# Seven block products for two node tiles in a relational graph layer, x kept in DRAM meanwhile, and eight buffers for the edge network

## The chip, the cores and the metric

The kernel runs on one core of a Trainium2 chip. The metric is device microseconds of one execution. The engines have these names in the profile: PE is TensorE (matrix products; PEld its loads of the stationary operand), DVE is VectorE, ACT is ScalarE, POOL is GpSimd, SP is SyncE, which issues most of the transfers here.

## What is computed (the reference, cut)

A stack of four graph layers ("blocks" 0 to 3) works on 1024 nodes with 512 features each and on 17408 edges, which are sorted by target node. Every layer first normalizes x and adds its result to x or replaces it. Block 0 is a convolution with a normalized adjacency matrix, block 1 multiplies gathered node features with weights that a small network makes for each edge (three products with SiLU between them), block 2 is a Chebyshev convolution. Block 3 is the one that the larger part of the change is about, a relational convolution, applied twice:

```python
def _rel_graph_conv(h, src, dst, etypes, norm, basis, comp, bias, loop_w, apply_relu):
    hb = jnp.einsum('nd,bdo->bno', h, basis)          # 4 bases of 512 x 512
    coef = comp[etypes]
    m = coef[:, 0, None] * hb[0][src]
    for b in range(1, basis.shape[0]):
        m = m + coef[:, b, None] * hb[b][src]
    m = m * norm[:, None]
    agg = jax.ops.segment_sum(m, dst, num_segments=n)
    out = agg + bias + h @ loop_w
    return jax.nn.relu(out) if apply_relu else out
```

The kernel changes the order: it sums the gathered rows of h for each basis first, and multiplies the sums with the bases afterwards. For a tile of 128 nodes that product is (128 x 2048) with (2048 x 512): 4 bases of 4 chunks of 128 each.

## The kernel before, in words

The code decides at run time between two arms, stack(True) and stack(False); the data of the runs takes the first (`fast`). All arithmetic that matters here is in float32. Instructions are traced in program order and then ordered by a planner, which lets an instruction go ahead when by its own cost estimates its inputs and buffers are ready; the order on each engine is then fixed. `pinned` and `issue_after` hold it to the traced order in places. A write at a place that is known only at run time counts as touching the whole tile.

**The edge network (L427 to L504).** `hidden` takes a batch of 1024 edges through three products (L434), each followed by a SiLU on ACT (L436) into a buffer of the tag `hid`, of which there are four. The third output is written to the table `hidtab` in DRAM (L438). Thirteen batches run two at a time (`in_turns`), one product between two groups of the loop that counts edges (L500, L504); the other four run later. The tiles for weights and edge data that later blocks need (`ew`, `ea`, `comps`, `w_mlp4`, `w_out0` and others, L106 to L118) lie in the pool `const` for the whole run; `load_rest` (L120) loads them.

**Rows.** `bias_row` (L93) loads a row of 512 numbers to all partitions. Rows share a tag of four buffers in `wpool`. Big weights (1 MB, `load_w`, L88) share another tag with four buffers there.

**Block 2** ends in `prop2` (L915): for each node tile, x is updated, normalized to h3, and h3 is written to the table `htabs[0]` (L919). `loop0` (L924) makes h @ loop_w plus the bias for a tile into `hb`, the tile `stage`.

**Block 3, layers l = 0 and 1 (L978 on).** The edges are cut into 68 groups of 256 (G = 2 times 128). For each group:

- `gathered` (L1001, gather at L279) fetches 2 x 128 rows of `htabs[l]` by indirect transfers that POOL issues, up to 11 buffers ahead;
- `weighted` (L1010) makes one-hot rows times coefficients on DVE (L1013);
- 8 products of 128 columns (16 instructions, L1027) sum the rows for four bases and a window of 32 nodes in a PSUM buffer `ps`, of which there are four;
- DVE adds them to `sums` (L1043), a tile [128, 4 chunks, 4 bases, 1024 nodes], at a column that is read from memory (`base(g)`).

Since the edges are sorted, a node tile n is complete when group `settled(n)` is through: 11, 19, 28, 36, 45, 53, 62 for tiles 0 to 6, and the end of the loop for tile 7. From then on `products` (L967) multiplies it with the four bases, 16 products of 512 columns (L972) into one PSUM bank, at most two products to a group; what is left runs after the loop (L1044). `ready` (L955) adds the result to `hb` (layer 0) or to x (layer 1). In layer 0 it then applies the relu on ACT, writes the tile to `htabs[1]` (L960) and lets POOL clear the tile's part of `sums` (L962); in layer 1 it writes the result out (L965).

In the first groups of either layer the loop products fill TensorE: tiles 3 to 7 of `loop0`, or of `turned5` and `loop1`, in groups 0, 1, 2, 4 and 6 (L1029). `loop1` adds into x on DVE and then the bias row on POOL (L990). Layer 1 begins with its weights (L980: loop weight, three bases, row; the fourth base at L982), whose buffers come free as layer 0's products finish with theirs, and with tiles 0 to 2 of `loop1`.

Of the kernel before, what the change touches and what calls it, by code (L numbers as in the profile page):

```python
# [21 lines left out]
P = 128  # L22
# [17 lines left out]
NY = 5  # L40
# [9 lines left out]
def gnn_stack(ctx, tc, a, out, xtab, htabs, hidtab):  # L50
# [42 lines left out]
    def bias_row(name, key):  # L93
        r = wpool.tile([P, D], F32, tag="row", name=f"row_{key}")
        nc.sync.dma_start(r, row_bcast(a[name], D))
        return r
# [8 lines left out]

    ew = const.tile([P, ET], F32, name="ew")  # L106

    ea = const.tile([P, ET, NY], F32, name="ea")

    comps = const.tile([P, 2, 8, NBAS], F32, name="comps")  # L110
    w_mlp2 = const.tile([P, P], F32, name="w_mlp2")
    w_mlp3 = const.tile([P, P], F32, name="w_mlp3")

    w_mlp4 = const.tile([P, 2, 4 * MUL], F32, name="w_mlp4")
    w_up0 = const.tile([P, MUL], F32, name="w_up0")
    w_up1 = const.tile([P, MUL], F32, name="w_up1")
    w_out0 = const.tile([P, 2, MUL], F32, name="w_out0")
    w_out1 = const.tile([P, 2, MUL], F32, name="w_out1")  # L118

    def load_rest():  # L120
        for t, key in ((w_up0, "L1_gnn_W_up0"), (w_up1, "L1_gnn_W_up1"), (w_mlp4, "L1_gnn_W_mlp4"), (ea, "edge_attr_4"),
                       (ew, "edge_weight")):
            nc.sync.dma_start(t, a[key])
        for t, key in ((w_out0, "L1_gnn_W_out0"), (w_out1, "L1_gnn_W_out1")):
            nc.sync.dma_start(t, a[key].rearrange("(c p) o -> p c o", p=P))
        for l in range(2):
            nc.sync.dma_start(comps[:, l], a[f"L3_gnn_comp{l}"])

        nc.gpsimd.tensor_scalar(w_out0[:, 1, :], w_out0[:, 1, :], 1.0 / math.sqrt(3.0), None, op0=ALU.mult)
# [233 lines left out]
    def stack(fast):  # L363
# [24 lines left out]

        cpool_cm = tc.tile_pool(name=f"cpool{fast}", bufs=1)
# [54 lines left out]
        def in_turns(batches):  # L444

            batches = list(batches)
            for i in range(0, len(batches), 2):
                pair = batches[i : i + 2]
                for _ in range(3):
                    for steps in pair:  # L450
# [4 lines left out]
                                 lambda q, i: l0.tile([P, 512], F32, tag="hid", name=f"hid_{q}_{i}", bufs=4))  # L455
# [386 lines left out]
        with tc.tile_pool(name=f"l2{fast}", bufs=1) as l2:  # L842
# [6 lines left out]
            b1 = bias_row("L2_gnn_b1", f"b1{fast}")  # L849
            gamma = bias_row("L2_gnn_gamma", f"gamma{fast}")  # L850
            beta = bias_row("L2_gnn_beta", f"beta{fast}")
            b2 = bias_row("L2_gnn_b2", f"b2{fast}")
# [90 lines left out]
        with tc.tile_pool(name=f"l3{fast}", bufs=1, reuse_waits="tile") as l3:  # L943
# [23 lines left out]
            def products(l, n, w3):  # L967

                po = bank2(f"po3_{l}_{n}")[:, 0, :]
                for b in range(NBAS):  # L970
                    for c in range(KC):
                        nc.tensor.matmul(po, sums[:, c, b, n * P : (n + 1) * P], w3[1 + b][:, c, :],  # L972
                                         start=(b == 0 and c == 0), stop=(b == NBAS - 1 and c == KC - 1))
                        if b == NBAS - 1 and c == KC - 1:
                            ready(l, n, po)
# [158 lines left out]
```

## Time and profile before

| what | value |
|---|---|
| median of 3 runs | 1245.97 us (1245.72 to 1247.47) |
| the profiled execution | 1234.54 us |
| its span (first to last instruction) | 1232.7 us |
| granted TensorE clock, mean | 0.997 |
| PE busy between 740 and 1230 us | nearly without a break |
| block 3, from the first group to the end | 712.7 to 1232.7 us |
| products with the bases in the chain that ended last | 17.8% of the span |
| edge groups (L1027) in that chain | 18.8% |

How to read the lines that follow in the prediction. The busy row gives for each engine its busy time, its share of the span and its number of instructions. The chain is followed backwards from the last instruction, at each step to whatever released it; in order of time its rows give start, length and what it was, "x8" meaning eight instructions in a row. A row of a group of instructions gives line, engine, operation, output and inputs with their shape and number, then busy time and the mean duration of one in ns, then idle time before them and what ended most of it. Durations of single matmuls overlap, so the distance from one start to the next is taken from rows with many in a row. A row of the waits gives who waited for whom, microseconds in total, times, and the longest. A row of the timeline gives start, length, engine, line, operation and form; an idle time before it stands in brackets.

### The profile page before, as it was taken

To read this page: it belongs to the slowest core of one execution; us is meant where nothing else is said; L and a number is where in the kernel's file an instruction comes from. 1 tells how busy PE (TensorE), PEld (TensorE's weight loads), DVE (VectorE), ACT (ScalarE), POOL (GpSimd) and SP (SyncE) were. 2 spreads that over 40 slices of the span, in tenths; PEclk is the share of its full clock that TensorE was granted. 3 is DMA by queue.
4 is the path that set the end of the run, shared out by engine and by line. 5 is a ranking of instruction groups with operands and counts; after the bars stand their busy time and mean duration, and the time that the engine had idled before them with its cause. 6 is when DMAs were issued, how large, how long until landed. Compare 5 with 4: busy or idle time off the path is not lost.

```text
span 1232.7 us, 17256 instructions
## 1 busy us (share of the span) xinstructions
PE 1203.1 (98%) x6338; PEld 799.5 (65%) x6354; DVE 617.2 (50%) x1180; ACT 291.2 (24%) x686; POOL 520.0 (42%) x596
## 2 busy tenths in 40 slices
PE   7988999999999999999999999999999999999998
PEld 3434567777777778544444567777776577777774
DVE  6877747777777676435443443333332143333331
ACT  4346254444444443322222400000000000000000
POOL 2000445666666662100000166565661486555530
PEclk9999999999999999999999999999999999999999
DMA  5171035444444441002002267555551666555540
GB/s 192 33 253 61 18 130 148 134 137 137 136 130 137 137 129 35 1 9 77 0 1 92 79 182 219 159 167 156 169 155 52 213 199 197 163 165 169 160 129 18
DMA packets 55620, 150.31 MB, mean 122 GB/s; under 512 B 8612, under 2 KB 10088, under 8 KB 55400
## 3 DMA queue, kind: packets, MB, share of 16 engines
q0 software_dynamic: 32640, 106.98, 30.3%
q1 hardware_dynamic: 22600, 41.63, 10.1%
q8 instruction: 52, 0.85, 0.3%
q10 hardware_dynamic: 288, 0.52, 0.1%
q14 instruction: 40, 0.33, 0.1%
HBM read 136.25 MB, written 12.85 MB: 121 GB/s over the span
## 4 chain that ended last, share of the span: by engine, by line
PE 93%; DMA 3%; ACT 1%; DVE 1%; issue 1%; POOL 1%; SPq 0%; ACTq 0%; DVEq 0%; POOLq 0%
PE ps L1027 19%; PE po L972 18%; PE pg L812 14%; PE pu L262 10%; PE pw L752 10%; PE pz L238 7%; PE py L238 4%; PE pl L238 4%; PE pm L434 3%; DMA hidtab_dram<-hid 2%; PE po L736 1%; PE pt_l L228 1%; PE pc L500 1%; PE pup L622 1%; PE pt_c L228 1%
## 5 line engine op out<-in xcount | busy, mean ns | idle before, releaser
L279 POOL DMA_INDIRECT m<-htab_dram,src_i x272 | 260.0, 956 | 167.4 <-PE ps L1027 115.9
L1027 PEld LDWEIGHTS ps<-wo,m 128*128 128x128 f32 x2176 | 261.5, 192 | 57.9 <-issue 56.2
L1027 PE MATMUL ps<-wo,m 128*128 128x128 f32 x2176 | 262.3, 275 | 1.0 <-DMA m<-htab_dram,src_i 1.0
L812 PEld LDWEIGHTS pg<-yo,msg 128*128 128x128 f32 x1632 | 192.8, 192 | 32.0 <-issue 16.3
L812 PE MATMUL pg<-yo,msg 128*128 128x32 f32 (+1 forms) x1632 | 187.8, 272 | 0.0
L1043 DVE TENSOR_TENSOR sums<-sums,ps 128x512 f32 x136 | 93.6, 688 | 157.3 <-PE po L972 133.8
L769 ACT ACTIVATE dot<-s,ea 128x128 f32<-128x128 f32 x408 | 130.0, 390 | 160.2 <-DVE msg L774 133.6
L279 POOL DMA_INDIRECT s<-xtab_dram,src_i x136 | 131.9, 970 | 37.3 <-issue 26.3
L752 PE MATMUL pw<-w_mlp,hq 128*128 128x512 f32 x272 | 133.3, 612 | 0.0
L1013 DVE TENSOR_TENSOR wo<-ohw,cwTrue 128x256 f32<-128x256 f16 x136 | 63.5, 469 | 103.5 <-PE ps L1027 103.5
L792 POOL TENSOR_TENSOR yo<-ohw,ea 128x160 f32<-128x160 f16 x136 | 63.2, 486 | 72.7 <-PE pg L812 72.7
L262 PE MATMUL pu<-parts,cnt 128*128 128x512 bf16 x373 | 84.1, 379 | 0.5
L953 POOL MEMSET sums<- 128x4096 f32 x1 | 3.5, 3512 | 165.8 <-PE pu L262 165.8
L752 PEld LDWEIGHTS pw<-w_mlp,hq 128*128 128x128 f32 x272 | 46.6, 191 | 33.5 <-issue 33.2
L262 PEld LDWEIGHTS <-cnt 128*128 128x128 f16 x384 | 37.6, 98 | 45.9 <-issue 3.4
L770 DVE TENSOR_TENSOR msg<-pw,s 128x512 f32<-128x512 f32 x68 | 47.0, 692 | 39.2 <-PE pw L752 36.4
L771 DVE TENSOR_TENSOR msg<-s,pw 128x768 f32<-128x768 f32 x68 | 64.2, 944 | 0.0
L972 PE MATMUL po<-basis_0True,sums 128*128 128x512 f32 x128 | 60.8, 600 | 0.2
L972 PE MATMUL po<-basis_3True,sums 128*128 128x512 f32 x128 | 59.8, 594 | 0.8 <-DVE sums L1043 0.8
L972 PE MATMUL po<-basis_2True,sums 128*128 128x512 f32 x128 | 59.9, 593 | 0.0
L972 PE MATMUL po<-basis_1True,sums 128*128 128x512 f32 x128 | 59.9, 593 | 0.0
L959 ACT ACTIVATE stage<-stage 128x512 f32<-128x512 f32 x8 | 5.0, 630 | 226.8 <-DVE stage L958 226.8
(175 smaller groups left out, 1284.0 us busy)
## 6 DMA issues: line engine op xcount, KB each, us to landing
hq<-hidtab_dram SPq DMA_DIRECT2D x17, 256.0 KB, 3.0
m<-htab_dram,src_i POOLq DMA_INDIRECT x272, 3.6
hidtab_dram<-hid SPq DMA_DIRECT2D x13, 256.0 KB, 4.1
s<-xtab_dram,src_i POOLq DMA_INDIRECT x136, 3.5
xtab_dram<-up SPq DMA_DIRECT2D x8, 256.0 KB, 2.0
basis_0True<-in_L_gnn_basis_dram SPq DMA_DIRECT2D x2, 1024.0 KB, 5.1
basis_1True<-in_L_gnn_basis_dram SPq DMA_DIRECT2D x2, 1024.0 KB, 5.2
htab_dram<-hl SPq DMA_DIRECT2D x8, 256.0 KB, 2.0
```

The source lines that it names most:

```text
L238: ins = nc.tensor.matmul(pz, hT[:, c, :], w[:, c, :], start=(c == 0), stop=(c == KC - 1)).ins
L262: nc.tensor.matmul(pu, m[:, s, d * P : (d + 1) * P], z[:, s, :], start=(s == 0 and j == 0), stop=(s == NB - 1 and j == len(zs) - 1))
L279: nc.gpsimd.indirect_dma_start(out=g, out_offset=None, in_=table, in_offset=bass.IndirectOffsetOnAxis(ap=idx[:, t : t + 1], axis=0))
L752: nc.tensor.matmul(pw[:, k, :], hq[q][:, (t % 4) * P : (t % 4 + 1) * P], w_mlp4[:, t // 4 % 2, :], start=True, stop=True)
L769: nc.scalar.activation(dot[:, k, m, :], s1[:, k, m, :], AF.Copy, scale=ea[:, g * G + k, 1 + m : 2 + m])
L771: nc.vector.tensor_mul(msg[:, :, 2:5, :], s1, w[:, :, 2:3, :].to_broadcast([P, G, 3, MUL]))
L792: nc.gpsimd.tensor_mul(yo[:, k], ohw[:, t, :].unsqueeze(1).to_broadcast([P, NY, W]), ea[:, t, :].unsqueeze(2).to_broadcast([P, NY, W]))
L812: nc.tensor.matmul(ps[:, b : b + n, :], lhsT, rhs, start=(k == 0), stop=(k == G - 1))
L972: nc.tensor.matmul(po, sums[:, c, b, n * P : (n + 1) * P], w3[1 + b][:, c, :], start=(b == 0 and c == 0), stop=(b == NBAS - 1 and c == KC ...
L1013: nc.vector.tensor_mul(wo, ohw[:, ts, :].unsqueeze(2).to_broadcast([P, G, NBAS, W]), cw[:, l, ts, :].unsqueeze(3).to_broadcast([P, G, NBAS ...
L1027: nc.tensor.matmul(ps[:, c * P : (c + 1) * P], m[k][:, c * P : (c + 1) * P], wo[:, k].rearrange("p b w -> p (b w)"), start=(k == 0), stop= ...
L1043: nc.vector.tensor_add(part, part, ps.rearrange("p (i w) -> p i w", w=W))
```

## The change

Five things are changed.

1. **Seven block products for two node tiles.** Two node tiles are taken together (`pair_products`). Their sums are a block matrix of two by two: rows are the two tiles, columns are bases 0 and 1, and bases 2 and 3. The bases are a block matrix of two by two too: rows are bases 0 and 1, and 2 and 3; columns are the left and the right 256 features. The product of the two is made by seven block products with sums and differences of blocks (the Winograd form of Strassen's scheme), not by eight. A block product is 2 bases x 4 chunks = 8 products of 256 columns. The differences of the bases (`Right.make`: t1 to t4, eight subtractions of 128 x 1024 a layer) are made once per layer on DVE, one to a group after group 8 (layer 0) or 10 (layer 1). t1 and t2 lie in the place of x (layer 0) or hb (layer 1), t3 overwrites a block of the bases, t4 has a tile. For each pair DVE makes s1, s2, s3 and s4 (128 x 1024 each; s3 and s4 overwrite blocks of `sums`) and adds every block product to one to four of the four result blocks.
2. **When the steps run.** A pair is begun when its second tile is settled (groups 19, 36, 53, and the end), and its 56 steps are spread evenly over the groups up to the next pair's beginning (`due`). The loop products move to groups 0, 2, 5, 8 and 11. `sums` is cleared for two tiles at a time; the last pair's part in group 4 of layer 1.
3. **x in DRAM.** In the fast arm `prop2` also writes x to `xtab`, and after the fourth block product of layer 0's last pair x is read back in eight transfers of 256 KB.
4. **Eight network buffers.** `hid` has eight buffers, not four.
5. **Places.** The tiles for weights and edge data move from `const` to a pool `early`, which is closed before block 3. The four rows of block 2 lie in block 2's pool `l2`; the tag of the other rows has two buffers. Layer 1's loop weight is asked for in group 12 of layer 0.

The diff, cut to its core:

```diff
-                                 lambda q, i: l0.tile([P, 512], F32, tag="hid", name=f"hid_{q}_{i}", bufs=4))
+                                 lambda q, i: l0.tile([P, 512], F32, tag="hid", name=f"hid_{q}_{i}", bufs=8 if fast else 4))
...
-            b1 = bias_row("L2_gnn_b1", f"b1{fast}")
+            b1 = bias_row("L2_gnn_b1", f"b1{fast}", l2)
...
                 h3[d] = normed(d, "l3")
+                if fast:
+                    nc.sync.dma_start(xtab[d * P : (d + 1) * P, :], x[:, d, :])
                 nc.sync.dma_start(htabs[0][d * P : (d + 1) * P, :], h3[d])
...
+            def cleared(p):
+                for n in (2 * p, 2 * p + 1):
+                    nc.gpsimd.memset(sums.rearrange("p c b d -> p (c b) d")[:, :, n * P : (n + 1) * P], 0.0)
...
+                def make(self):
+                    for b in range(HB):
+                        for out, x0, x1 in ((self.t1, self.block(0, 1), self.block(0, 0)), (self.t2, self.block(1, 1), self.t1),
+                                            (self.t3, self.block(1, 1), self.block(0, 1)), (self.t4, self.block(1, 0), self.t2)):
+                            nc.vector.tensor_sub(out(b), x0(b), x1(b))
+                            yield
+
+            PAIR = 7 * HB * KC
+
+            def pair_products(l, p, right):
+                a11, a12, a21, a22 = (left(p, i, j) for i in range(2) for j in range(2))
+                s1, s2 = (l3.tile([P, KC, HB, P], F32, tag=f"s{k}", name=f"s{k}_{l}_{p}") for k in (1, 2))
+                nc.vector.tensor_add(s1, a21, a22)
+                nc.vector.tensor_sub(s2, s1, a11)
+                s3, s4 = a21, a12
+                nc.vector.tensor_sub(s3, a11, a21)
+                two = bank2(f"po3_{l}_{p}")
+
+                h = (hb, x)[l][:, 2 * p : 2 * p + 2, :].rearrange("p i (k q) -> p (i k) q", k=2)
+                every, last3, lower, odd = slice(0, 4), slice(1, 4), slice(2, 4), slice(1, 4, 2)
+                for step, (lhs, rhs, places) in enumerate((
+                        (a11, right.block(0, 0), every), (a12, right.block(1, 0), slice(0, 1)), (s2, right.t2, last3), (s1, right.t1, odd),
+                        (s3, right.t3, lower), (s4, right.block(1, 1), slice(1, 2)), (a22, right.t4, slice(2, 3)))):
+                    ps = two[:, step % 2, step // 2 % 2 * H : (step // 2 % 2 + 1) * H]
+                    for b in range(HB):
+                        for c in range(KC):
+                            nc.tensor.matmul(ps, lhs[:, c, b, :], rhs(b)[:, c, :], start=(b == 0 and c == 0),
+                                             stop=(b == HB - 1 and c == KC - 1))
+                            if b == HB - 1 and c == KC - 1:
+                                part = h[:, places, :]
+                                nc.vector.tensor_add(part, part, ps.unsqueeze(1).to_broadcast([P, part.shape[1], H]))
+                                if step == 1:
+                                    nc.vector.tensor_sub(s4, a12, s2)
+                                if step == 3 and l == 0 and p == NB // 2 - 1:
+                                    for n in range(NB):
+                                        nc.sync.dma_start(x[:, n, :], xtab[n * P : (n + 1) * P, :])
+                                if step == 5:
+                                    ready(l, 2 * p)
+                                if step == 6:
+                                    ready(l, 2 * p + 1)
+                                    if l == 0 and p < NB // 2 - 1:
+                                        cleared(p)
+                            yield
+
+            since = [settled(2 * p + 1) for p in range(NB // 2 - 1)] + [NG]
+
+            def due(g):
+                return sum(max(0, min(PAIR, (g - a + 1) * PAIR // (b - a))) for a, b in zip(since, since[1:]))
...
-                        todo = (step for n in range(NB) for step in products(l, n, w3))
+                        right = Right(w3, (x, hb)[l], l)
+                        making = right.make()
+                        todo = (step for p in range(NB // 2) for step in pair_products(l, p, right))
...
-                            n = {0: 3, 1: 4, 2: 5, 4: 6, 6: 7}.get(g)
+                            n = {0: 3, 2: 4, 5: 5, 8: 6, 11: 7}.get(g)
...
-                            done = sum(settled(n) <= g for n in range(NB - 1))
-                            for _ in range(2):
-                                if given < done * NBAS * KC:
-                                    next(todo)
-                                    given += 1
+                            if l == 0 and g == 12:
+                                w3_1 = loop_weights(1)
+                            if l == 1 and g == 4:
+                                cleared(NB // 2 - 1)
+                            if g > 8 + 2 * l:
+                                next(making, None)
+                            while given < due(g):
+                                next(todo)
+                                given += 1
                             part = sums.rearrange("p c b d -> p (c b) d")[:, :, bass.ds(base(g), W)]
                             nc.vector.tensor_add(part, part, ps.rearrange("p (i w) -> p i w", w=W))
```

## The prediction

> **What bounds the kernel now.** I read the busy row first, then the chain that ended last, then the costliest groups.
>
> ```profile
> PE 1203.1 (98%) x6338; PEld 799.5 (65%) x6354; DVE 617.2 (50%) x1180; ACT 291.2 (24%) x686; POOL 520.0 (42%) x596
> ...
> PE 93%; DMA 3%; ACT 1%; DVE 1%; issue 1%; POOL 1%; SPq 0%; ACTq 0%; DVEq 0%; POOLq 0%
> ...
> L279 POOL DMA_INDIRECT m<-htab_dram,src_i x272 | 260.0, 956 | 167.4 <-PE ps L1027 115.9
> ...
> L972 PE MATMUL po<-basis_0True,sums 128*128 128x512 f32 x128 | 60.8, 600 | 0.2
> ```
>
> TensorE is the bound: 93% of the chain is its instructions, and it waits only some 25 us in all. So a microsecond of TensorE work taken out is a microsecond gained, unless TensorE then waits for something that its own work covers today. The gather row (L279) waits 115.9 us for TensorE: gathers are ahead, not late. The busy means (600 ns) overlap, so I take pitches from the chain in order of time, where only the extension counts:
>
> ```profile
> 56.94 7.22 DMA hidtab_dram<-hid
> ...
> 701.69 3.44 PE pl L238 x8
> ...
> 742.54 8.93 PE ps L1027 x80
> ...
> 947.38 17.35 PE po L972 x40
> ...
> 966.13 4.10 DMA htab_dram<-stage
> 973.55 3.68 DMA m<-htab_dram,src_i
> ```
>
> A product of 128x512 is two instructions of 3.44/8 = 430 ns; at 128 columns an instruction takes 8.93/80 = 111.6 ns. One edge group (L1027, 16 instructions) is thus 1.79 us, and a group with two products of L972 is 1.79 + 4 x 0.43 = 3.51 us.
>
> **Part 1, seven products for eight.** Removed: 2 layers x 8 tiles x 16 products = 512 instructions of 512 columns, 512 x 0.430 = 220.2 us (the chain has 17.8% of 1232.7 = 219.4). Added: 2 x 4 pairs x 56 products of 256 columns = 896 instructions. The trace has no f32 instruction of 256 columns. Below: half the 512 row, 215 ns; above: twice the 128 row, 223 ns. I take the line through both rows, 111.6 + 128 x (430 - 111.6)/384 = 217.7 ns, since both rows have a common overhead. 896 x 0.2177 = 195.1 us. **Gain 25 us**, bounds 20 (at 223) and 27.5 (at 215).
>
> The row at 512 columns is 430 ns against 111.6 at 128, so it is nearly in proportion to the columns. [...]
>
> **Part 2, eight network buffers.** The waits of TensorE and ScalarE before 102 us:
>
> ```profile
> PE pm L434 <- ACT hid L436: 7.0, 5, 2.7
> ```
> ```profile
> ACT hid L436 <- DMA hidtab_dram<-hid: 11.3, 4, 4.1
> ```
>
> TensorE's waits there are 2.00, 2.73 and 1.30 us, each behind a ScalarE output whose buffer is still being written to DRAM, and twice 0.46 in the odd last batch, which stay. A buffer comes round after 4 outputs, 4 x 1.08 = 4.3 us, and the write takes up to 7.2; with 8 it comes round after 8.7. **Gain 6.0 us.** VectorE is next: 37.7 us busy of 50 there, so the shorter stage (about 47 us of 53) still has room; bounds 3 and 6.
>
> **Part 3, tiles moved, rows in another pool, x through DRAM.** The early tiles' loads wait for the setup pool, finished before the branch: 0. The four bias rows now load after the last message group (478 us); the first is read after the product at 496.5 us, and a row lands in 3 to 6 us: 0, at most 2. x is written to DRAM eight times (256 KB, 2.0 us to landing) on SP, each ahead of the table write that layer 0's gathers wait for. The last is free 2.5 us before that write (704.69 us) and shares the engines with the basis_3 load issued at 699.45: 0.5 us, bounds 0 and 2.
>
> **Part 4, layer 0's groups.** Products now begin at group 19, not 11, so the gathers' pitch of 1.254 us (2.51 a group) against 1.79 could show. First gather 707.64, so the two of group 18 have landed at 707.64 + 37 x 1.254 + 3.68 = 757.7. TensorE starts group 0 at 712.7 and gets to group 18 after 18 x 1.79 + 5 loop products x 3.44 = 49.4, at 762.1. No stall. From 19 on a group has 3.29 steps of 2 x 0.2177: 1.79 + 1.43 = 3.22 us, over 2.51.
>
> Ahead of the first pair, VectorE makes the combined bases, 8 subtractions of 1024 elements (1.2 us each by the row fit below) from group 9 on (11 in layer 1). With the add (0.69) and the wo multiply (0.42) a group then takes VectorE about 2.1 us against 1.79; five such groups put it 1.6 us behind, which the four PSUM buffers of ps hide. Three of the eight need basis_2, whose load waits for the last loop product (issued at 742.57 today, landing in up to 9.0); that moves to 751.7 and lands by 761, ahead of group 21 (some 768), where the first product with it stands. Cost 0; up to 5 if VectorE's order has one of the three ahead of the adds.
>
> What is new in the loop is serial: each group's add into sums must follow that group's steps, and the next steps must follow that add, since the add's place is known only at run time. Memsets of sums stand in the same line, as today:
>
> ```profile
> 806.70 1.82 POOL L962 MEMSET sums<- 128x2048 f32 x1
> ```
> ```profile
> 808.55 1.41 DVE L1043 TENSOR_TENSOR sums<-sums,ps 128x512 f32 x2
> ```
> ```profile
> 806.00 3.96 PE L1027 MATMUL ps<-wo,m 128*128 128x128 f32 x34
> 810.01 1.98 PE L972 MATMUL po<-basis_0True,sums 128*128 128x512 f32 x4
> ```
>
> The add ran the moment the memset ended (808.52); TensorE filled the time with 34 instructions of later groups. For a pair the line is 17 x (steps 1.43 + end 0.16 + add 0.69 + restart 0.15) = 41.3; plus s1 to s3, 3 x 1.2 (rows 0.42, 0.69, 0.94 at 256, 512, 768 elements; 1.2 at 1024) less overlap, 3.4; s4 1.1; seven adds from PSUM 4.3; in layer 0 two memsets, 2 x 1.82 and their start, 4.2. That is 50.1 us in layer 1 and 54.3 in layer 0, against TensorE's 17 x 1.79 + 112 x 0.2177 = 54.8. TensorE stays the bound, narrowly. At a pair's end in layer 0, memset, add and s1 to s3 outlast three groups of cover (5.4 us, four PSUM buffers) by about 0.7 us: 2 x 0.7, and 1 for the first pair's start in each layer's loop and the rest: **2.5 us lost**, bounds 0 and 6 x 3.7 = 22 (no cover).
>
> Third pair, layer 0: it ends in the last group, so the memsets stand before the last add and the last pair's first product with no groups left: 2 x 1.82 + 0.69 + 0.2 = 4.5, less some transposes as cover: **4 us lost**, bounds 0 and 4.5. The last 56 steps then run back to back, 24.4 us, with s1 to s3 (3.4) under the first two products (7 us).
>
> **Part 5, between the layers.** Today the last product ends at 964.56, the table write is issued at 966.13, lands at 970.2, and gathering begins at 972.28. The 4 MB of weights had been issued 3.43 us apart, each landing in 5.1 to 5.4: no backlog. After the change 2 MB of x start 24 steps (10.4 us) before the end, then 1 MB each at 8.7, 6.9, 5.2 and 3.5 us before it. At some 390 GB/s (the best slices between 945 and 985 us show 385 to 408) 6 MB need 16 us, so the write waits to about 8.6 us after the end, not 5.6: **3 us lost**, bounds 0 and 8. The next layer's three loop products (11.6 us) cover the first part today and keep doing so.
>
> Layer 1's POOL also has the eight adds of the bias row (1.28 us) and, at group 4, the two memsets moved there, 1.68 each over a gather's pitch (805.75 to 808.68 less 1.25). Gather 37 is issued today at 1027.03, 54.75 after the first; with 3.4 for memsets and 3.68 to land, 61.8. TensorE without waiting gets to group 18 at 978.94 - 972.28 + 17 x 1.79 + 5 x 3.44 + 4 x 0.43 = 56.0. Products that today start at group 11 no longer cover this. 5.8, and some 0.2 more at group 19: **6 us lost**, bounds 2 and 9.
>
> **Sum**, against the profiled execution (1234.54, span 1232.7 and 1.8 around it): -25 - 6 + 0.5 + 2.5 + 4 + 3 + 6 = -15, so 1219.5. The runs' median, 1245.97, lies 0.9% above that execution; in proportion, 1245.97 x 1219.5/1234.54 = **1231 us**.
>
> **Rivals.** (a) The waits are covered: the order of the instructions fills them with later groups, as at 806 us. For it: only 1.0 us of waiting for gathers in all of today's trace. Against it: in layer 1 there is no work to fill with. 25 + 6 less 2 to 6: 1216 to 1221. (b) Slower: VectorE's line in the group loop becomes the bound. Place: groups 19 to 67 of both layers. Its margin is 0.5 us a pair in layer 0 and 4.7 in layer 1; each 0.1 us more per group adds 1.7 us a pair. At 0.5 us more (a wo multiply of 0.42, row L1013, in front of every add) a pair costs 8 in layer 0 and 3.8 in layer 1, 3 x 11.8 = 35, so 15 of gain turn into 20 of loss: 1266. It decides from about 0.3 us a group. For it: VectorE is busy 60% of the loop and serves in order. Against it: the multiply can run under TensorE's steps, as it does now. (c) The change doesn't do what it says: a 256-column instruction at 245 ns makes the products as dear as now; 6 less 16 is 10 lost, 1256. Both rows speak against it.
>
> **How the numbers follow.** Forecast 0.55 (own range 1222 to 1242), (a) 0.25, (b) 0.14, (c) 0.04, and 0.02 for a forecast that ends at no change. Range 1214 to 1247: from (a) with the low bound of part 1 to the forecast with part 5 at its high bounds (5 and 3 more) and 6 more in the loop; most of (b) and (c) is left out. Faster by over 0.2% (about what a measurement of this kernel can tell from no change) 0.80, within 0.04, slower 0.16.
>
> **What would show it.** Pitch of the new products at 215 to 223 ns; no wait of ScalarE for hidtab and pa starting near 96 us; memset, add and product in a row at layer 0's last pair, with TensorE idle some 4 us; layer 1's TensorE waiting for gathers around groups 12 to 19; the last htab write landing over 5 us after its issue. Wrong if TensorE idles within groups 20 to 66, behind the adds of sums.

## The result, and the profile after

The changed kernel takes 1268.03 us (median, 1265.27 to 1269.26) against 1246.20 for the kernel before in the same session: a ratio of 1.017, interval 1.015 to 1.019. It is slower by 1.7%; the forecast was 1231 us and faster.

The profile that came with this result, its busy row and the engines' shares of the chain:

```profile
PE 1197.9 (95%) x6722; PEld 883.0 (70%) x6738; DVE 691.5 (55%) x1268; ACT 291.1 (23%) x686; POOL 529.4 (42%) x596
...
PE 89%; DMA 4%; DVE 2%; issue 1%; ACT 1%; POOL 1%; another core or an unknown queue 0%; SPq 0%; ACTq 0%; DVEq 0%; POOLq 0%
```

TensorE is busy 5 us less than in the profile before (1197.9 against 1203.1), and the span is 32.4 us longer (1265.1 against 1232.7). So the products did become cheaper, and TensorE waits where it didn't wait before.

The two profiles can't be subtracted from one another, though. The runs fell on chips of two kinds: on some the kernel before takes about 1246 us, on others about 1236, and the profile that I predicted from (1234.5) is of the second kind while the three times shown beside it, and the profile after, are of the first. So I took both kernels once more on one chip of the second kind (c1_before, c2_after). There the medians are 1235.83 and 1246.24, and the changed kernel has a ratio of 1.0082 (1.0057 to 1.0108) to the kernel before: slower on that kind too, by 9 to 10 us. The readings below are of this pair unless they say otherwise. The busy rows, before and then after:

```profile
PE 1204.7 (98%) x6338; PEld 799.9 (65%) x6354; DVE 617.7 (50%) x1180; ACT 291.0 (24%) x686; POOL 517.7 (42%) x596
```
```profile
PE 1191.1 (96%) x6722; PEld 878.5 (71%) x6738; DVE 694.9 (56%) x1268; ACT 291.0 (23%) x686; POOL 529.2 (43%) x596
```

TensorE's work in block 3 can be counted from pitches: 112 instructions of 256 columns in a row take 24.43 us (a row shown under the first experiment), and in the undisturbed middle of that row 32 of them take 6.90 us from the first start to the start that follows them (timeline of c3_own_psum):

```profile
1208.30 7.07 PE L1039 MATMUL po<-stage,s 128*128 128x256 f32 x32
1215.20 1.89 PE L1039 MATMUL po<-basis_0True,sums 128*128 128x256 f32 x8
```

That is 0.2156 us from start to start; the sums here are made with 0.2155. The 896 new ones are 193.1 us, the 512 old ones 220.2 at 0.430. What TensorE's starts are apart beyond those pitches is waiting, or half clock. By stretch, in us, from profiles on chips of the second kind (the last three columns are experiments, told below):

| stretch of block 3 | before (c1) | changed (c2) | own PSUM (c3) | and VectorE clears (e6) | plain products (c8) |
|---|---|---|---|---|---|
| layer 0, groups 0 to 18 | 0.0 | 2.6 | 5.2 | 2.5 | 0.0 |
| layer 0, groups 19 to 66 | 2.2 | 6.3 | 3.8 | 3.8 | 0.4 |
| layer 0, last pair, and into layer 1 | 0.1 | 7.9 | 3.6 | 3.6 | 0.7 |
| layer 1, groups 0 to 18 | 0.9 | 12.4 | 13.4 | 5.0 | 6.8 |
| layer 1, groups 19 to 66 | -0.1 | 4.1 | 1.2 | 1.7 | 1.1 |
| layer 1, last pair | 1.0 | 8.3 | 1.7 | 1.7 | 1.7 |
| sum | 4.1 | 41.7 | 28.9 | 18.2 | 10.6 |

Before to changed: 27.1 us less work, 37.6 us more waiting, and block 3 begins 1.5 us earlier: +9.0, against +8.7 in the spans (1233.8 and 1242.5). The 1.5 is within what executions differ by: block 3 begins at 714.2 us in c1_before and at 712.7 and 713.1 in the two other profiles of the kernel before, and at 712.7 in c2_after. The gain is there in full, and more than that is lost to waits. Where the waits stand is read from the chain of c2_after at its end (start, length, what):

```profile
1207.68 3.71 PE po L1039 x16
...
1211.48 1.23 DVE x L1043
1212.71 0.04 issue
1212.76 3.73 PE po L1039 x16
...
1216.52 0.43 DVE x L1043
1216.95 0.04 issue
1216.99 3.73 PE po L1039 x16
1220.73 0.02 issue
1220.75 0.96 DVE x L1043
1221.71 0.04 issue
1221.76 3.73 PE po L1039 x16
```

Each block product (16 instructions) ends, VectorE adds it to one to four result blocks (0.43 to 1.23 us), and only then does the next one start. The rows of the waits sum this up (who waited for whom, total, times, longest):

```profile
PE po L1039 <- DVE x L1043: 5.1, 6, 1.4
...
PE pm L436 <- ACT hid L438: 4.9, 4, 3.2
PE po L1039 <- DVE stage L1043: 4.4, 5, 1.3
PE ps L1115 <- DVE sums L1135: 3.7, 1, 3.7
```

9.5 us stand in front of block products in the two last pairs. The row of `pm` shows that the wait for network buffers is still there with eight of them (6.1 us before). The last row is a wait in layer 1 that is read below.

### The profile page after: what moved, and what is told of

Read it like the earlier page. It is cut to its first block, busy times and chain, and to the rows that moved or that the text cites. A ratio compares the mean times of both kernels' runs of the same rounds, so it can differ in the third digit from the quotient of the medians.

```text
span 1265.1 us, 18143 instructions
## 1 busy us (share of the span) xinstructions
PE 1197.9 (95%) x6722; PEld 883.0 (70%) x6738; DVE 691.5 (55%) x1268; ACT 291.1 (23%) x686; POOL 529.4 (42%) x596
## 4 chain that ended last, share of the span: by engine, by line
PE 89%; DMA 4%; DVE 2%; issue 1%; ACT 1%; POOL 1%; another core or an unknown queue 0%; SPq 0%; ACTq 0%; DVEq 0%; POOLq 0%
PE ps L1115 19%; PE po L1039 16%; PE pg L814 14%; PE pu L237 10%; PE pw L754 10%; PE pz L213 7%; PE py L213 4%; PE pl L213 4%; PE pm L436 2%; PE po L738 1%; PE pt_l L203 1%; DMA types<-in_edge_type_dram 1%; DMA m<-htab_dram,src_i 1%; DMA hidtab_dram<-hid 1%; POOL sums L987 1%
## 5 line engine op out<-in xcount | busy, mean ns | idle before, releaser
L254 POOL DMA_INDIRECT m<-htab_dram,src_i x272 | 269.2, 990 | 159.1 <-PE ps L1115 100.9
L1115 PEld LDWEIGHTS ps<-wo,m 128*128 128x128 f32 x2176 | 269.3, 194 | 29.5 <-issue 8.9
L1115 PE MATMUL ps<-wo,m 128*128 128x128 f32 x2176 | 272.5, 278 | 15.0 <-remote 3.5
L794 POOL TENSOR_TENSOR yo<-ohw,ea 128x160 f32<-128x160 f16 x136 | 63.4, 488 | 72.3 <-PE pg L814 72.2
L1099 DVE TENSOR_TENSOR wo<-ohw,cwTrue 128x256 f32<-128x256 f16 x136 | 59.6, 440 | 49.0 <-PE ps L1115 41.8
L817 DVE TENSOR_TENSOR acc<-acc,pg 128x256 f32 x68 | 28.7, 422 | 48.5 <-PE pg L814 48.5
L1039 PE MATMUL po<-basis_0True,sums 128*128 128x256 f32 x128 | 33.7, 396 | 14.1 <-DVE sums L1135 11.1
L237 PE MATMUL pu<-parts,adj 128*128 128x512 bf16 x187 | 42.1, 379 | 3.7 <-ACT parts L244 2.3
L1039 PE MATMUL po<-basis_2True,sums 128*128 128x256 f32 x128 | 34.8, 400 | 7.5 <-issue 2.5
```

The costliest lines, as they stand in the source:

```text
L237: nc.tensor.matmul(pu, m[:, s, d * P : (d + 1) * P], z[:, s, :], start=(s == 0 and j == 0), stop=(s == NB - 1 and j == len(zs) - 1))
L254: nc.gpsimd.indirect_dma_start(out=g, out_offset=None, in_=table, in_offset=bass.IndirectOffsetOnAxis(ap=idx[:, t : t + 1], axis=0))
L794: nc.gpsimd.tensor_mul(yo[:, k], ohw[:, t, :].unsqueeze(1).to_broadcast([P, NY, W]), ea[:, t, :].unsqueeze(2).to_broadcast([P, NY, W]))
L1039: nc.tensor.matmul(ps, lhs[:, c, b, :], rhs(b)[:, c, :], start=(b == 0 and c == 0), stop=(b == HB - 1 and c == KC - 1))
L1099: nc.vector.tensor_mul(wo, ohw[:, ts, :].unsqueeze(2).to_broadcast([P, G, NBAS, W]), cw[:, l, ts, :].unsqueeze(3).to_broadcast([P, G, NBAS ...
L1115: nc.tensor.matmul(ps[:, c * P : (c + 1) * P], m[k][:, c * P : (c + 1) * P], wo[:, k].rearrange("p b w -> p (b w)"), start=(k == 0), stop= ...
```

## The experiments

Theory A: the products are cheaper as computed, and the waits have separate causes, which can be taken away one by one: (1) the PSUM buffer that a pair's seven block products share, (2) the combined bases that VectorE makes in order and the late load they need, (3) the two memsets in layer 1's group 4 and late gathers there. The rivals stand in the expectations.

**e1_own_psum**, a PSUM buffer for each block product:

```diff
-                two = bank2(f"po3_{l}_{p}")
...
-                    ps = two[:, step % 2, step // 2 % 2 * H : (step // 2 % 2 + 1) * H]
+                    ps = bank2(f"po3_{l}_{p}_{step}")[:, 0, :H]
```

> Each block product gets a PSUM buffer of its own (two in turn) in place of a quarter of one buffer per pair. Theory A (the waits in front of block products come from the shared buffer: a block product may not start before VectorE's add of the previous one): the waits behind the adds of L1043 go, 4.4 us in layer 0's last pair, 5.1 in layer 1's, 1.2 at the second block product of two pairs, so 11 to 13 us less than the changed kernel, ratio to the kernel before about 1.007. Rival (the waits are for something else of the previous block product, or the time is lost again behind other adds): under 3 us less, ratio 1.015 or more.

Measured: 1250.63 us, ratio 1.0044 (1.0027 to 1.0062). That is 17 us less than the changed kernel in the first session, 16 by the ratios, and more than theory A had counted. Once more, as the base of three others, on a chip of the second kind:

> The kernel with a PSUM buffer of its own for each block product once more, as the base of the next three on one chip. It was 1.0044 of the kernel before on a chip where the changed kernel was 1.017; on a chip where the changed kernel is 1.008 it should be 0.995 (theory A: 16 us of waits behind the shared buffer, whatever the chip). Rival (the gain was the chip's): nearer to 1.004 than to 0.995 there.

Measured: 1230.93 us, ratio 0.995 (0.9934 to 0.9965); the changed kernel has 1.0082 on such chips, so again 16 us less. The chain at the end of c3_own_psum:

```profile
1201.32 24.43 PE po L1039 x112
```

Where c2_after had seven pieces with VectorE between them, there is one of 112 instructions. The waits that go in the table are 10.9 us in the last pairs and 5.4 in groups 19 to 66. (The span of c3_own_psum is only 13.0 us shorter than that of c2_after, since the first groups of either layer wait 3.6 us more there.) In the last pairs they are the pieces shown above. In the groups of c2_after they can't be pointed at: TensorE has just two longer waits in front of a block product there, 0.87 us each at the beginning of a pair, which stay with own buffers, and all others are at most 0.14 us. Only in the first profile of the changed kernel do two second block products wait visibly (1.27 and 1.19 us). For the last pairs the cause is shown: with a buffer of its own a block product doesn't wait for the add, and in the shared one it did, although it wrote to other columns than the add read.

**e2_late_making**, in layer 0 the three subtractions that need basis_2 behind the adds of groups 15, 16 and 17; the edit also lets all eight begin after group 17 in program order, not after group 8:

```diff
-                            nc.vector.tensor_sub(out(b), x0(b), x1(b))
+                            with tc.issue_after(added[14 + k].ins) if l == b == 0 < k else nullcontext():
+                                nc.vector.tensor_sub(out(b), x0(b), x1(b))
...
-                            if g > 8 + 2 * l:
+                            if g > (17 if l == 0 else 10):
...
+                            added.append(nc.vector.tensor_add(part, part, ps.rearrange("p (i w) -> p i w", w=W)))
```

> The three subtractions that need basis_2 in layer 0 are held behind VectorE's adds of groups 15, 16 and 17. Theory A (VectorE stands 4.2 us before the load of basis_2, with the adds of sums behind it, and TensorE runs dry and falls to half clock): TensorE's idle 3.5 us at 767 to 771 us and half of the 3.4 us at half clock go, 5 to 6 us less than the changed kernel, ratio about 1.012 to 1.013. Rival (that stretch is limited by gathers, so the time comes back before group 19): 0 to 2 us less, ratio 1.015 to 1.017.

Measured: 1274.53 us, ratio 1.0227 (1.0204 to 1.025), 6 us more than the changed kernel. Neither expectation held. In the changed kernel's first profile VectorE's idle time before the subtraction is 3.24 us, not 4.2. TensorE's idle 3.5 us at 770 us went (layer 0's groups 0 to 18 wait 8.4 us, not 11.9 as in the changed kernel's first profile), but groups 19 to 66 wait 24.1, not 12.6, 5.4 of them in one piece, at 799.9 us, for an add whose own release the profile doesn't name. This fell on a chip of the first kind, and the changed kernel's first profile, from that kind too, has such a piece as well (5.50 us before 1068.5); what the edit alone costs stays open.

**e3_hid4**, four network buffers again (`bufs=8 if fast else 4` to `bufs=4`), and once more beside its base:

> Part 2 undone: four network buffers. Theory A (the eight buffers brought 0.5 us, since ScalarE still waits for table writes that stand behind other loads): within 2 us of the changed kernel, ratio 1.015 to 1.019. Rival (they bring the 6 us that the prediction counted, and other stages ate it): 4 to 6 us more than the changed kernel, ratio 1.020 to 1.022.

> The changed kernel once more, as the base of the next two on one chip: 1.008 of the kernel before where semaphores come in time, 1.017 on a chip like the first.

> Part 2 undone once more, beside its base. Theory A (the table writes stand behind big loads with eight buffers too, so the wait only moves): within 2 us of the changed kernel. Rival (the 6 us of the prediction are there): 4 to 6 us more.

Measured: 1270.12 us, ratio 1.0203 (1.018 to 1.0226). In the second session the changed kernel has 1269.60, 1.0186 (1.0159 to 1.0213), and four buffers 1270.71, 1.0197 (1.0169 to 1.0225). The first ratio falls at the low end of the rival's range, but its interval reaches the changed kernel's; the second, taken side by side, is theory A's: 1.1 us.

In their own stage the eight buffers did bring something. `pa`, the first product behind it, starts at 97.3 to 101.2 us in the 13 profiles with eight buffers (mean 99.1) and at 101.4 to 102.7 in the five with four (mean 102.1). That is 3 us, half of the forecast. At the first product of the message groups, near 185 us, the means differ by only 1.2 us. What became of the rest of the wait can be read from the chains. Before (c1_before), then changed (c2_after):

```profile
56.93 7.12 DMA hidtab_dram<-hid
...
64.75 7.00 DMA hidtab_dram<-hid
```
```profile
57.12 13.03 DMA types<-in_edge_type_dram
70.16 4.88 DMA w_out<-in_L_gnn_W_out_dram
75.11 8.65 DMA hidtab_dram<-hid
```

With four buffers two table writes of 7 us hold ScalarE. With eight, ScalarE runs on, and what it then waits for is a later write. Two rows of c2_after:

```profile
SPq L385 <- DMA types<-in_edge_type_dram: 5.3, 1, 5.3
ACT hid L438 <- DMA hidtab_dram<-hid: 6.2, 2, 4.3
```

SyncE, which issues loads and table writes in one line, waits 5.3 us until a load has landed before it issues the next one. The write comes behind that one, takes 8.65 us, and ScalarE waits 4.3 us for it. Between 55 and 85 us the hardware queue's packets fill 82% of the 16 engines' time at 250 GB/s in the first profile before and 79% at 223 GB/s in the first profile after. That the queues are the limit there, and not the number of buffers, fits this, but no run tests it.

**e4_plain_pairs**, the schedule of the changed kernel (pairs, `due`, moved loop products, memsets, x in DRAM) with ordinary products; sums, differences and combined bases are left out:

```diff
-            PAIR = 7 * HB * KC
+            PAIR = 2 * NBAS * KC
...
+            def pair_plain(l, p, w3):
+                for n in (2 * p, 2 * p + 1):
+                    yield from products(l, n, w3)
...
-                        todo = (step for p in range(NB // 2) for step in pair_products(l, p, right))
+                        todo = (step for p in range(NB // 2) for step in pair_plain(l, p, w3))
```

> The schedule of the changed kernel (pairs from groups 19, 36, 53 and the end, moved loop products, memsets by pairs, x in DRAM) with ordinary products of 512 columns, 32 to a pair, without sums, differences and combined bases. Theory A (the seven products save 27 us of TensorE's time, and about 20 us of that are lost to waits that the block products bring with them, the rest of the loss being the schedule's): 220 - 193 = 27 more, 12 less for the shared PSUM buffer, 5 for the making, 3 for s1 to s3, so 5 to 9 us more than the changed kernel, ratio 1.021 to 1.025. Rival (the products as blocks save nothing on the chip, their extra work on VectorE is the whole loss): faster than the changed kernel by 10 us or more, ratio under 1.009.

> The schedule of the changed kernel with ordinary products of 512 columns, without sums, differences and combined bases, beside its base. Theory A (27 us less work by seven products, 16 us of which are lost to the shared PSUM buffer and some 5 to sums, differences and combined bases; the schedule alone costs some 15 us of waits): 4 to 8 us more than the changed kernel, ratio 1.011 to 1.015. Rival (the schedule costs next to nothing where semaphores come in time, the blocks' waits eat the whole gain): ratio 1.000 to 1.004, 5 us or more less than the changed kernel.

> The pair schedule with ordinary products once more. On a chip where the kernel before takes about 1237 us theory A expects a ratio of 1.011 to 1.015 (the schedule alone costs some 15 us), the rival 1.000 to 1.004. On a chip with 1246 us it is 1.016 again.

Measured: 1265.51 us, ratio 1.0168 (1.0144 to 1.0192), and 1266.07, 1.0159 (1.0131 to 1.0187), on chips of the first kind; 1240.31 us, 1.0039 (1.0023 to 1.0056), on one of the second. None of the three fell where theory A had it: I expected the schedule to cost some 15 us by itself, and on the second kind of chip it costs 5. There the rival of c8 held, 6 us less than the changed kernel: as written, the block products lose more than they save. That they save nothing on this chip, the rival of e4, is refuted by c3_own_psum, which is 9 us under plain products with the same schedule.

**e5_loops_early, e6_clear_dve, e7_both**, on own PSUM buffers. e5 puts the loop products back, e6 clears the last pair's part of `sums` on VectorE behind layer 0's last product, e7 does both:

```diff
-                            n = {0: 3, 2: 4, 5: 5, 8: 6, 11: 7}.get(g)
+                            n = {0: 3, 1: 4, 2: 5, 4: 6, 6: 7}.get(g)
```
```diff
-                                    if l == 0 and p < NB // 2 - 1:
-                                        cleared(p)
+                                    if l == 0:
+                                        cleared(p, nc.gpsimd if p < NB // 2 - 1 else nc.vector)
...
-                            if l == 1 and g == 4:
-                                cleared(NB // 2 - 1)
```

> Own PSUM buffers, and the loop products of tiles 3 to 7 back in groups 0, 1, 2, 4 and 6, as before the change. Theory A (the moved loop products hold the buffer that basis_2 needs; its load comes at group 12, stops the gathers for some 4 us and VectorE waits for it with the adds of sums behind it): basis_2 lands before VectorE asks for it, 3 to 5 us less than the base. Rival (the cover is only used up earlier, TensorE then waits for gathers before group 19): within 1 us of the base or slower.

> Own PSUM buffers, and the last pair's part of sums cleared for layer 1 by VectorE behind layer 0's last product, not by GpSimd in group 4 of layer 1. Theory A (GpSimd's two memsets, 3.6 us in the line of its gathers, hold the adds of sums at about group 7 and make the gathers late afterwards): TensorE's idle 3.7 us and the half clock behind it go, and part of the later waits for gathers, 6 to 10 us less than the base. Rival (layer 1 is bound by its gathers with or without the memsets): 0 to 3 us less.

> The last two together on own PSUM buffers. Theory A (three separate causes): the gains of both add up, 9 to 15 us less than the base, ratio to the kernel before 0.983 to 0.988 where the base has 0.995. Rival (both act on the same wait for gathers): no better than the better of the two by more than 1 us.

Measured against c3_own_psum (1230.93) on the same chip: 1229.31 us, ratio 0.9944 (0.9926 to 0.9962); 1225.05, 0.991 (0.9876 to 0.9944); 1223.93, 0.9901 (0.9883 to 0.9919). e6 is 6 us less by the medians, at the low end of what theory A had, though its interval and that of c3_own_psum overlap a little. What it takes away is read from the timeline of c2_after (start, length, engine, line, form, idle before it):

```profile
1000.71 3.56 POOL L987 MEMSET sums<- 128x2048 f32 x2
1004.31 1.41 DVE L1135 TENSOR_TENSOR sums<-sums,ps 128x512 f32 x2 [8.18 <-POOL sums L987]
...
1005.05 6.36 PE L1115 MATMUL ps<-wo,m 128*128 128x128 f32 x32 [3.72 <-DVE sums L1135]
```

The memsets stand behind gathers and a bias add in GpSimd's order and start at 1000.7; the add of a group, already computed, waits 8.2 us for them; the four PSUM buffers of `ps` fill, and TensorE idles 3.7 us. The 32 instructions that follow take 6.36 us, not the 3.6 of their pitch: the granted clock was 0.5 from 1003.5 to 1010.4 us. Without these memsets layer 1's groups 0 to 18 wait 5.0 us, not 13.4.

The memsets are only about half of what is lost there. Of the 12.4 us of c2_after, 6.5 are in groups 6 to 8, where the memsets stand, and 5.7 in groups 16 to 18. (The plain pairs of c8, with the same memsets, lose 5.5 in groups 6 to 8: that is most of what the schedule costs by itself.) In groups 16 to 18 it is the load of basis_2, in layer 1:

```profile
1032.36 1.23 DVE L1016 TENSOR_TENSOR stage<-basis_2True,stage 128x1024 f32<-128x1024 f32 x1 [2.96 <-DMA basis_2True<-in_L_gnn_basis_dram]
1036.89 7.22 PE L1115 MATMUL ps<-wo,m 128*128 128x128 f32 x48 [2.85 <-issue]
```

VectorE waits 2.96 us for the load and does three subtractions before the next add; TensorE idles 2.85 us, and the clock is at half for 3.41. In e6 VectorE still waits 2.6 us for the load, but TensorE by then waits for gathers (2.0 us at 1021); its waits in groups 15 and 16 are 3.9 us together.

e5 is 1.6 us less by the medians, between the two expectations and with intervals that overlap. What the load of basis_2 does in layer 0 is the same. VectorE of c2_after:

```profile
755.67 0.42 DVE L1099 TENSOR_TENSOR wo<-ohw,cwTrue 128x256 f32<-128x256 f16 x1
758.28 1.23 DVE L1016 TENSOR_TENSOR x<-basis_2True,x 128x1024 f32<-128x1024 f32 x1 [2.19 <-issue]
759.42 1.22 DVE L1016 TENSOR_TENSOR basis_0True<-basis_2True,basis_0True 128x1024 f32<-128x1024 f32 x1
760.56 1.22 DVE L1016 TENSOR_TENSOR t<-basis_2True,x 128x1024 f32<-128x1024 f32 x1
761.69 0.68 DVE L1135 TENSOR_TENSOR sums<-sums,ps 128x512 f32 x1
```

VectorE stands 2.2 us before the subtraction that needs basis_2, and does three in a row before the next add; TensorE, four PSUM buffers ahead, then idles 2.4 us. In e5 this is down to waits of 0.5 to 1.0 us, and layer 0's groups 0 to 18 wait 2.7 us, not 5.2. That is not shown to be a gain of e5: e6, whose layer 0 has the order of c3_own_psum, waits 2.5 us there, and c2_after 2.6. The 5.2 of c3_own_psum hold a longer idle piece (3.39 us) with half clock behind it.

In layer 1 the waits of e5 are fewer (8.8 against 13.4): GpSimd's memsets still hold an add there, for 3.2 us, but TensorE doesn't idle for it, and VectorE waits only 0.4 us for basis_2; 5.6 of the 8.8 are in groups 13 to 16, behind gathers.

e7 is better than e6 by 1.1 us, not by the sum. That is nearer to the rival: e5 and e6 both take away the waits in groups 6 to 8. Even the 1.1 isn't shown to come from the edit: the waits in block 3 are 19.6 us in the profile of e7 against 18.2 in that of e6, and its span is shorter because block 3 begins at 709.7 us, not 714.7, ahead of anything that differs.

e7 beats both kernels on that chip, by 1.0% against the kernel before. The kernel of e7 again, beside c4_after on a chip of the first kind (e8_plain_clear):

> Own PSUM buffers, early loop products and clearing by VectorE once more, beside the changed kernel on this chip: 22 us less than the changed kernel by theory A (16 for the buffers, 6 to 7 for the rest), ratio 0.990.

Measured: 1246.41 us, ratio 1.0014 (0.9995 to 1.0033): 23 us less than the changed kernel there, as expected, but no gain over the kernel before; the ratio of 0.990 that the expectation gave was missed. So whether the seven products pay, mended, depends on the chip.

**c1_before, c2_after, c7_before**, for second profiles:

> The kernel before once more, for a second profile: the first had 1234.5 us against a median of 1246. Theory A (that execution went on without a break in block 3 and others do not): a profile of about 1245 us with 5 to 10 us of TensorE's waiting or slow stretches in block 3 that the first did not have, which would take 10 us off what block 3 is charged with. Rival (the first profile is typical, the difference lies outside the profiled execution): again about 1234 us and no such stretch.

> The changed kernel once more, for a second profile. If the stretches in which TensorE's instructions come 0.7 us apart without a wait (at 729 us, and at 1060 us) belong to this order of instructions, they come again at the same places; if they are chance, they lie elsewhere or are gone and the profile is 5 to 10 us shorter.

> The kernel before, for a profile on whatever chip this is. On a chip where it takes about 1246 us, theory A expects the 9 us more in block 3, in stretches where groups follow each other without products (groups 6 to 11 of each layer), with the semaphores of TensorE arriving 0.7 us apart there. Rival: the 9 us lie outside block 3, as time from slower loads, and the changed kernel's 22 us more on such a chip are of another kind. On a chip with about 1237 us it shows nothing new.

Measured: 1235.83 us, ratio 1.0004 (0.9984 to 1.0024); 1246.24, 1.0082 (1.0057 to 1.0108); 1236.24, 1.0006 (0.9994 to 1.0018). The profiles of before are again near 1234 us and without such stretches, so the first was typical of its kind of chip. c7 fell on the second kind as well, so the kernel before has no profile on the first kind, and its 9 us there stay unlocated.

## Why the prediction was wrong, by its own steps

- **Part 1, 25 us of products.** Right: 27.1, at the bound that half the 512 row gives (215 ns).
- **Part 2, 6 us by eight buffers.** Wrong: 3 at the end of the stage, 1 to 2 in the whole. The failing step was "with 8 it comes round after 8.7". It set the buffers' turn against a write of up to 7.2 us that is issued as soon as its output is there; in c2_after the write was issued behind loads of 13.03 and 4.88 us and then took 8.65, and ScalarE waited 4.3 us for it.
- **Part 4, the last pair: "The last 56 steps then run back to back, 24.4 us".** This is the step that failed most. They took 31.1 us in layer 1 (1207.68 to 1238.79). The seven products share one buffer of two banks. The prediction has no term for that, so it takes the buffer's quarters as independent, and it counts the adds on VectorE's side only, 4.3 us a pair. In the last pairs it costs 10.9 us, and with the groups, by their sum alone, 5.4 more. Without the shared buffer the 56 steps do take 24.43 us.
- **Part 4, the group loop, 2.5 us.** 8.3 measured, and 2.9 with own PSUM buffers. So the line of add, steps and add is priced about rightly without the shared buffer; the two waits at the beginning of a pair are 0.9 us each, 0.7 was forecast. Rival (b), VectorE's line as the bound with 35 us lost, is not what c2_after shows; that 1268 us lies beside its 1266 is luck.
- **Part 4, making the bases, "Cost 0; up to 5".** 2.6 us in layer 0, by the way that was named for the upper end: three that need basis_2 ahead of the adds. In layer 1 the same again, 5.7 us with the half clock behind it, which the prediction had at nothing there.
- **Part 4 and 5, 4 us at layer 0's last pair and 3 between the layers.** The sum, 7.8, is near by accident: 1.8 us are the memsets and the last add, most of the rest was the shared buffer, and nothing was lost between the layers: in c2_after TensorE went from its last block product into transposes and loop products without a break, and the first gathered rows of layer 1 were in time.
- **Part 5, layer 1's groups, 6 us (bounds 2 and 9).** 11.5, and hardly any of it by the late gathers that were forecast (one wait of 0.8 us); those show in e5 and e6, when the other waits are gone. I let the two memsets only delay the gathers. First of all they hold up the adds, 6.5 us in groups 6 to 8, the very line (add behind memset) that the trace of before showed at 806 us, and around the idle piece lie 6.83 us at half clock, which the sum had not priced at all. The other 5.7 us are those of basis_2.
- **The level.** I scaled the profile's 1219.5 by 0.9% to the median of the three runs, as if the difference were spread evenly. It was a difference between chips.

The sum by steps, in us: -25, -6, +0.5, +2.5, +4, +3 and +6 were forecast, together -15; measured were -27.1, -1.5 (with the writes of x in it), +8.3 in the groups, +7.8 at layer 0's end, +11.5 and, forecast at nothing, +2.6 and +7.3: together +8.9. Of the 24 us between, the shared PSUM buffer is 16. The point that I named as what would make the prediction wrong, TensorE idle behind the adds of sums within groups 20 to 66, was not where it broke on the second kind of chip: 1.7 us in two pieces. In the profile that came with the result it is 8.8 us, most of it in one piece in layer 1:

```profile
PE po L1039 <- DVE sums L1135: 5.5, 1, 5.5
```

The add that TensorE waited for had itself waited 2.2 us for something that the profile doesn't name, so the sign was there, but its cause isn't known.

On the chips of the first kind the changed kernel loses 13 us more. There its profile has 63.4 us of waiting in block 3 (41.7 on the second kind), and that of the plain pairs 36.5 (10.6); the difference lies in the groups. The plain pairs lose as much, so it doesn't take the block products. It is described below and not explained.

## What to carry to other kernels

When a tile in PSUM is cut into parts for several results, ask what the waits are attached to: here a block product into a part that no one read still waited for the reader of its neighbour (10.9 us in the two last pairs of c2_after), and a buffer for each result, two in turn, took the wait away (112 instructions in 24.43 us without a break in c3_own_psum). The order on each engine is fixed, and in c2_after one add held everything behind it on VectorE for 8.2 us because two memsets ahead of it were late; so the thing to look for, ahead of busy shares, is which addition or memset stands between a finished product and the next free PSUM buffer. And work that covered a thin stretch is part of the price of moving it: 37.6 us of new waits came from an engine that was 98% busy.

## What the runs showed of the hardware

**Half clock around short idle pieces.** The granted clock fell to 0.5 for 6.83 us from 1003.5 us in c2_after, around an idle piece of 3.72, and for 3.41 us behind one of 2.85 at 1037; c3_own_psum has 3.41 us behind an idle piece of 3.39 at 764, c2_after none behind 2.42 at 763. The idle pieces of 2.85 and 3.39 us are shorter than the 3.41 that follow, and smaller ones have it around them too: e5_loops_early has 3.41 us from 973.6 around waits of 1.33 and 0.82, e6_clear_dve none around 1.33 and 0.81 at the same place. The first profile of the changed kernel has stretches of the same two lengths in block 3: 6.83 us from 731.4, 3.41 from 772.3 and 6.83 from 1065.9. The first of them lies around idle pieces of 0.76, 0.35 and 1.16 us, so the length of the pieces alone doesn't decide it.

**Chips of two kinds.** On three chips the kernel before took 1235 to 1237 us and the changed kernel, where it ran, 1246; on two others, and in the first session, whose chip isn't on record, 1246 and, where it ran, 1268 to 1270. In the slower profiles TensorE's instructions come 0.7 us and more apart, without a wait that the profile shows, in stretches where groups follow each other without products. In the first profile of the changed kernel, and then the same place in c2_after:

```profile
725.73 2.95 PE L1115 MATMUL ps<-wo,m 128*128 128x128 f32 x25
729.44 0.36 PE L1115 MATMUL ps<-wo,m 128*128 128x128 f32 x1 [0.76 <-issue]
730.15 0.27 PE L1115 MATMUL ps<-wo,m 128*128 128x128 f32 x1 [0.35 <-issue]
731.58 1.31 PE L1115 MATMUL ps<-wo,m 128*128 128x128 f32 x3 [1.16 <-issue]
```
```profile
724.91 5.52 PE L1115 MATMUL ps<-wo,m 128*128 128x128 f32 x48
```

The place comes again in c4_after (729.49) and e1_own_psum (729.16), so it belongs to the order of the instructions on that kind of chip. In the same profiles fewer updates of TensorE's semaphore are recorded (2219 in the first profile after, 2385 in c2_after), and some of them in bursts (eleven within 0.5 us at 733 us of the first profile after). Whether the semaphores themselves or their recording are slow there, these runs don't tell.

**Gathers while a load lands.** While basis_2 (1 MB, issued at 760.7 us) was landing, the gathers' queue moved nothing for 3 us, from 762 to 765 us in the first profile after, though GpSimd went on issuing gathers (at 761.2, 762.5 and 763.7 us). The first profile before has the same dip, with next to nothing moved from 745 to 747 us, but there TensorE had gathered rows and products in hand and did not wait: it is busy in all 38.6 us from 712.7 to 751.3.
